# Gate O moves from the bank of I and F into the bank of G in the last LSTM steps, and the edge targets are loaded once

## The chip, the cores and the metric

The kernel runs on one core of one Trainium2 chip. TensorE (PE in the profile, with its weight loads as PEld), VectorE (DVE), ScalarE (ACT), GpSimd (POOL) and SyncE (SP) each work through a queue of their own in order, and wait for each other on counters (semaphores). The metric is the device time of one execution in microseconds; of a kernel, the median of its runs is taken.

## The reference

One layer of a graph network on 6250 nodes of 256 features with 100000 edges, all in float32. `x` is normalised, then three branches add up:

```
xn = layernorm(x)
x  = x + GIN(xn, src, dst) + MIX(xn)      # segment_sum(xn[src], dst), two matmuls, batch norm; linear attention, two matmuls
x  = x + FFN(layernorm(x))                # an LSTM over the 6250 rows, hidden size 256

def step(carry, xp):                      # the LSTM
    h, c = carry
    i, f, g, o = split(xp + h @ W_hh.T, 4)
    c = sigmoid(f) * c + sigmoid(i) * tanh(g)
    h = sigmoid(o) * tanh(c)
```

The LSTM's outputs then give logits, an argmax, and weighted prefix and suffix sums that are added to the outputs. `dst` is sorted.

## The kernel before, in words

**The start (lines 204 to 343).** Nodes are laid out as 125 chunks of 50 steps. `x` comes in six groups of steps (`LN_GROUPS`, L223, two DMAs each by `move`, L118) on SP's queue, is normalised on DVE, ACT and POOL (L270 to L296), and is written to `xn_d` in DRAM, again on SP's queue (L296). The edges are loaded on ACT's queue (L208 to L216): `src` and `dst` each as a tile of `rows_e` rows of `EP` = 7 blocks of 128 edges, 112 rows of 896, in the buffer `behind`, a part of the large buffer that is called "counts" in the profile. The last row has no more than 5 real blocks; one DMA (L215) fills the other two. PE turns these tiles so that each block of 128 edges is one column (`edges_to_partitions`, L239: an integer-to-float copy on ACT, 7 transposes, two copies). The targets are needed a second time in another shape, 98 rows of 1024 (two groups of 512 edges each), for the smallest and largest target of each group (`ends`, L321) and of each pair (`pairs`, L333). For this `dst` is loaded again on SP's queue (L225 to L230, six DMAs into `flat`, a part of `m2`). These stand in SP's queue after the loads of `x` and before the stores of `xn_d`. A DMA that is issued waits until the one that used the same of eight counters, eight DMAs before it over SP and ACT, has landed.

After that POOL gathers rows of `xn_d` by `src` (L376, 646 gathers of 128 rows); the first one waits for all stores of `xn_d`. The iota of L362 (392 columns, in "counts") is copied to PSUM by ACT (L364) and used at L371 and L609.

**The LSTM.** The 125 chunks run side by side, 50 steps each. After 40 warm-up steps and the first 10 real ones (L1180 to L1208), the real steps from `KEPT` = 10 to 49, 40 of them, are run by an order written by hand (L1235 to L1282: `manual_schedule`, in which PE, DVE and ACT keep the order of the code). The input parts of the gates of these steps lie in DRAM; SP fetches one step's three steps ahead (`fetch`, L1120).

Gates and features are split into two halves `a` of 128 features, and so is h (`k`). A step makes 16 products (`products`, L1229): for each gate and half `a`, one with each half `k` of the last h. They add to input parts that `bring` (L1221) has placed in PSUM beforehand: by PE for the first steps, then by copies on ACT. There are six tiles in PSUM: `bank_g[a]` for G alone, `pg_g` in the profile, and `bank_o[s % 2][a]` for I, F and O, `pg` in the profile, in two sets that change with the step. The order of a step on PE is: six products with h's half 0; G, I, F, O of half 0 with h's half 1; then the rest of half 1; then the logits of the step before (L954). On ACT: tanh of G half 0 (L1254), sigmoid of I, F and O of half 0 in one instruction of 375 columns (L1256), tanh of G half 1 (L1258), the next step's copy into `bank_g[0]`, tanh of c half 0 (L1268), sigmoid of I, F, O of half 1, the copies into `bank_g[1]` and `bank_o[1]`, and tanh of c half 1. On DVE, for each half: the multiply of I, F with G, c (L1265), the add (L1266), a weighted sum of an earlier step (L959), and h = o * tanh(c) (L1271); after half 1 also the sums over the outputs (L963, L968, L959). The first product of the next step waits for h half 0 (L1271), the seventh for h half 1.

In the warm-up and the first ten steps (`step`, L1125) all four gates of a half lie in one PSUM tile and ACT reads them one by one (L1140).

Of the kernel before, what the change touches and what calls it, by code (L numbers as in the profile page):

```python
# [14 lines left out]
F32 = mybir.dt.float32  # L15
I32 = mybir.dt.int32
BF16 = mybir.dt.bfloat16
AF = mybir.ActivationFunctionType
# [5 lines left out]
P = 128  # L24
N, D, E = 6250, 256, 100000


NC, NS = 125, 50
HEADS, HC = 8, 32
KD = D // P  # L30
NE = -(-E // P)


GT, W = 4, 96
GROUPS = -(-NE // GT)
GE = GT * P
# [54 lines left out]
def gps_layer(ctx: ExitStack, tc: tile.TileContext, x, src, dst, cols, rows, kvln, wqkv, mw1, mw2, gw1, gw2,  # L91
              wih, whh, blstm, out):
    nc = tc.nc
# [38 lines left out]
    m2 = big.tile([P, 2 * BANK * KD], F32, name="m2", tag="M2")  # L132
# [11 lines left out]
    with ExitStack() as s1:  # L144
# [3 lines left out]
        def edges_flat(t, start, ap):  # L148
            return bass.AP(tensor=t.tensor, offset=t.offset + start, ap=ap)


        EP = 7
        rows_e = -(-NE // EP)
        si = wp.tile([P, rows_e * EP], I32, name="si")
        base_i = wp.tile([1, GROUPS], I32, name="base_i")
# [47 lines left out]

        with tc.tile_pool(name="ln1", bufs=2) as lp, tc.tile_pool(name="ps0", bufs=6, space=PSUM) as ps:

            tiled = []
            left = NE - (rows_e - 1) * EP
            for i, t in enumerate((src, dst)):  # L208
                s = behind[:, i * EP * P:(i + 1) * EP * P].bitcast(I32)
                for r0, r1 in ((0, 96), (96, rows_e - 1)):  # L210
                    nc.scalar.dma_start(s[r0:r1], edges_flat(t, r0 * EP * P, [[EP * P, r1 - r0], [1, EP * P]]))
                nc.scalar.dma_start(s[rows_e - 1:rows_e, :left * P],
                                    edges_flat(t, (rows_e - 1) * EP * P, [[left * P, 1], [1, left * P]]))
                if left < EP:
                    nc.scalar.dma_start(s[rows_e - 1:rows_e, left * P:], edges_flat(t, 0, [[P, 1], [1, (EP - left) * P]]))  # L215
                tiled.append(s)  # L216

            rows_g = GROUPS // 2
            real = E - (rows_g - 1) * 2 * GE
            last = E - (GROUPS - 1) * GE  # L220
            flat = m2[:, :2 * GE].bitcast(I32)
            dg = flat.rearrange("p (j e) -> p j e", j=2)
            for s0, n in LN_GROUPS:  # L223
                move(nc.sync, xn[:, s0:s0 + n, :], by_step(x)[:, s0:s0 + n, :])
            nc.sync.dma_start(flat[:96, :], edges_flat(dst, 0, [[2 * GE, 96], [1, 2 * GE]]))  # L225
            nc.sync.dma_start(flat[96:rows_g - 1, :], edges_flat(dst, 96 * 2 * GE, [[2 * GE, rows_g - 97], [1, 2 * GE]]))
            nc.sync.dma_start(flat[rows_g - 1:rows_g, :real], edges_flat(dst, (rows_g - 1) * 2 * GE, [[real, 1], [1, real]]))
            for at in range(real, 2 * GE, last):
                n = min(last, 2 * GE - at)
                nc.sync.dma_start(flat[rows_g - 1:rows_g, at:at + n], edges_flat(dst, E - n, [[real, 1], [1, n]]))  # L230
            nc.gpsimd.iota(iota, pattern=[[1, W]], base=0, channel_multiplier=0,
                           allow_small_or_imprecise_dtypes=True)
            nc.gpsimd.iota(place, pattern=[[1, 2]], base=0, channel_multiplier=2,
# [4 lines left out]
            with tc.manual_schedule(engines={mybir.EngineType.PE, mybir.EngineType.DVE, mybir.EngineType.Activation}):  # L238
                def edges_to_partitions(i):  # L239

                    to = (si, drel)[i].rearrange("p (q j) -> p j q", j=EP)
                    f = m1[:, i * EP * P:(i + 1) * EP * P]

                    nc.scalar.copy(f[:rows_e], tiled[i][:rows_e])
                    for j0 in range(0, EP, 4):
                        n = min(4, EP - j0)
                        pt = ps.tile([P, BANK], F32, name="mm")
                        pt = pt[:, :n * rows_e].rearrange("p (j q) -> p j q", q=rows_e)
                        for j in range(n):
                            nc.tensor.transpose(pt[:, j, :], f[:rows_e, (j0 + j) * P:(j0 + j + 1) * P],  # L250
                                                ident[:rows_e, :rows_e])
                        nc.scalar.copy(to[:, j0:j0 + n, :], pt)
# [98 lines left out]
        ps = s1.enter_context(tc.tile_pool(name="ps1", bufs=4, space=PSUM))  # L351
# [13 lines left out]
        to = [sums[:, k, :N].rearrange("p (c s) -> p s c", s=NS) for k in range(KD)]  # L365
# [439 lines left out]
        with tc.manual_schedule(engines={mybir.EngineType.PE, mybir.EngineType.DVE, mybir.EngineType.Activation}):  # L805
# [5 lines left out]
            while slot < GROUPS - COUNTED or running or before or any(s >= slot for s in starts):  # L811
                g = slot + COUNTED
# [31 lines left out]
        with tc.If(held < GROUPS + PAIRS, preferred_fallthrough_block=False):  # L844
# [15 lines left out]
            with tc.For_i(0, NE, 1) as c:  # L860
                at = edge_p.tile([P, 1], I32, name="at1")
# [3 lines left out]
                g = gather(at[:, :1])  # L865
# [50 lines left out]
    I, F, G, O = range(4)  # L916

    SLOT = {I: 0, F: 1, O: 2, G: 3}
# [10 lines left out]
    gc = wl.tile([P, KD, 2, NC], F32, name="gc")  # L929
# [111 lines left out]
    with tc.tile_pool(name="lstm", bufs=2) as rp:  # L1041
        AHEAD, FETCH = 3, 3
        s2 = ExitStack()
        ps = s2.enter_context(tc.tile_pool(name="ps3", bufs=4, space=PSUM))
# [170 lines left out]
        s2 = ExitStack()  # L1215
        ps = s2.enter_context(tc.tile_pool(name="ps_k", bufs=1, space=PSUM))
        ps_y = s2.enter_context(tc.tile_pool(name="ps_l", bufs=2, space=PSUM))
        bank_g = [ps.tile([P, NC], F32, name=f"pg_g{a}") for a in range(KD)]
        bank_o = [[ps.tile([P, SLOT[G], NC], F32, name=f"pg{i}{a}") for a in range(KD)] for i in range(2)]

        def bring(s, t, gate_g, a):  # L1221

            to, of = (bank_g[a], t[:, a, SLOT[G], :]) if gate_g else (bank_o[s % 2][a], t[:, a, :SLOT[G], :])
            if s < KEPT + (1 if gate_g else 2):
                nc.tensor.matmul(to, ident, of, start=True, stop=False, skip_group_check=True)
            else:
                nc.scalar.copy(to, of)

        def products(s, *of):  # L1229
            for g, a, k in of:  # L1230
                to = bank_g[a] if g == G else bank_o[s % 2][a][:, SLOT[g], :]
                nc.tensor.matmul(to, w_hh[:, k, block(g, a)], of_step(s - 1)[:, k, :], start=False, stop=(k == KD - 1),  # L1232
                                 skip_group_check=True)

        with tc.manual_schedule(engines={mybir.EngineType.PE, mybir.EngineType.DVE, mybir.EngineType.Activation}):  # L1235
            t = fetched.pop(0)
            for gate_g in (False, True):
                for a in range(KD):
                    bring(KEPT, t, gate_g, a)
            fetched.append(fetch(KEPT + FETCH))  # L1240
            w = None
            for s in range(KEPT, NS):
                more = s + 1 < NS
                t = fetched.pop(0) if more else None
                if more:
                    bring(s + 1, t, False, 0)
                products(s, (G, 0, 0), (I, 0, 0), (F, 0, 0), (O, 0, 0), (I, 1, 0), (F, 1, 0))
                products(s, (G, 0, 1), (I, 0, 1), (F, 0, 1), (O, 0, 1))
                products(s, (G, 1, 0), (G, 1, 1), (O, 1, 0), (I, 1, 1), (F, 1, 1), (O, 1, 1))
                pl = ps_y.tile([P, BANK], F32, name="pl")[:, :NC]  # L1250
                logits(s - 1, pl)
                for a in range(KD):
                    if a == 0:
                        nc.scalar.activation(gc[:, 0, 0, :], bank_g[0], AF.Tanh)  # L1254
                    gates = rp.tile([P, 4, NC], F32, name="gates")[:, :SLOT[G], :]
                    nc.scalar.activation(gates, bank_o[s % 2][a], AF.Sigmoid)  # L1256
                    if a == 0:
                        nc.scalar.activation(gc[:, 1, 0, :], bank_g[1], AF.Tanh)  # L1258
                    if more:
                        bring(s + 1, t, True, a)  # L1260
                    if a and more:
                        bring(s + 1, t, False, 1)

                    two = rp.tile([P, 2, NC], F32, name="two", tag="h_w")
                    nc.vector.tensor_mul(two, gates[:, :2, :], gc[:, a])  # L1265
                    nc.vector.tensor_add(c[:, a, :], two[:, 0, :], two[:, 1, :])  # L1266
                    t_c = rp.tile([P, NC], F32, name="t_c")
                    nc.scalar.activation(t_c, c[:, a, :], AF.Tanh)  # L1268
                    if w is not None:
                        weighted(s - 2, 0, w, a)  # L1270
                    nc.vector.tensor_mul(of_step(s)[:, a, :], gates[:, SLOT[O], :], t_c)  # L1271
                if more:
                    w = summed(s - 1, rp, pl)
                else:
                    gated_part(s - 1, last_w[:, 0], pl)
                if s + 1 + FETCH < NS:
                    fetched.append(fetch(s + 1 + FETCH))
            for k in range(KD):
                weighted(NS - 2, 2, inc, k)
            pl = ps_y.tile([P, BANK], F32, name="pl")[:, :NC]  # L1280
            logits(NS - 1, pl)
            gated_part(NS - 1, last_w[:, 1], pl)  # L1282
# [38 lines left out]
    with tc.If(right < 2 * D * (NC - 1), preferred_fallthrough_block=False):  # L1321
# [12 lines left out]
        with tc.For_i(0, NC, 1) as c0:  # L1334
# [3 lines left out]
            pg = ps.tile([P, NG, NS], F32, name="pg1")  # L1338
# [96 lines left out]
```

## Time and profile before

| | |
|---|---|
| median of 17 runs | 1682.35 us (1678.57 to 1686.9) |
| the profiled execution | 1680.71 us, of which the span is 1678.9 us |
| PE busy | 1454.9 us, 87% of the span |
| DVE, ACT, POOL busy | 927.8, 650.6, 697.0 us |
| mean granted clock of PE | 0.939 |
| the last 40 LSTM steps | from 1450 to 1638 us of the span |
| first gather issued | 59.34 us |

The page lists, for each group of instructions, the line of the kernel, the engine, what is written from what, the count, the busy time with the mean duration of one in ns, and the idle time before the group with what ended it. Matmuls in float32 take two passes, so the 640 products of L1232 are 1280 instructions there. The timeline gives start and duration in us; in brackets the idle time of the engine before the instruction, and who ended it. The chain of waits follows the work back from what ended last.

### The profile page before, as it was taken

The page shows a single profiled execution, that of the slowest core. Times are in us where ns is not written, and L with a number is a line of the kernel's source. Part 1 is how long each engine was busy: PE and PEld are TensorE (multiplying, and loading weights), DVE is VectorE, ACT ScalarE, POOL GpSimd, SP SyncE. Part 2 cuts the span into 40 slices and gives each one's busy share as a digit, 9 for nine tenths or more (in the row PEclk, how much of TensorE's full clock was granted, in tenths as well). Part 3 has the DMA queues.
Part 4 walks back from the last instruction along what each step waited for, and adds up shares of the span by engine and source line. Part 5 has one row for each costly group of instructions (what it writes and reads, how often), then busy time and mean ns, then how long its engine had stood idle before and what let it go on. Part 6 is the DMA issues. An engine that isn't in the chain of part 4 may idle for free.

```text
span 1678.9 us, 30496 instructions
## 1 busy us (share of the span) xinstructions
PE 1454.9 (87%) x11064; PEld 1383.9 (82%) x11064; DVE 927.8 (55%) x2923; ACT 650.6 (39%) x1917; POOL 697.0 (42%) x752
## 2 busy tenths in 40 slices
PE   2478888988887888988988889799999999999995
PEld 2467787887787788887888888799999999988884
DVE  5577677777773122212222213566667665688887
ACT  4432333333330122212322222566666653466660
POOL 5466666666666666666566664000000000000006
PEclk9689899899998899999999999899999999999996
DMA  9623332233234344433333333211111110133324
GB/s 231 224 88 89 89 88 86 86 89 88 87 88 143 114 127 130 127 104 105 95 102 101 104 101 120 76 75 63 75 62 75 63 51 1 50 111 111 111 74 155
DMA packets 63623, 165.98 MB, mean 99 GB/s; under 512 B 14415, under 2 KB 27943, under 8 KB 62460
## 3 DMA queue, kind: packets, MB, share of 16 engines
q0 software_dynamic: 31008, 84.71, 17.1%
q1 hardware_dynamic: 32016, 78.37, 14.2%
q8 instruction: 91, 1.49, 0.4%
q10 hardware_dynamic: 436, 0.81, 0.2%
q14 instruction: 72, 0.59, 0.1%
HBM read 130.56 MB, written 33.28 MB: 98 GB/s over the span
## 4 chain that ended last, share of the span: by engine, by line
PE 68%; DVE 12%; issue 10%; ACT 4%; DMA 2%; another core or an unknown queue 2%; POOL 1%; SPq 1%; DVEq 0%; POOLq 0%; ACTq 0%
PE pg L397 15%; PE pg L1107 11%; PE pg L1131 10%; PE mm L582 6%; PE pg L1232 4%; PE mm L593 4%; PE mm L422 3%; PE mm L543 3%; PE sums_c L737 2%; PE mm L554 2%; PE pg_g L1232 2%; ACT gates L1256 1%; DVE counts L622 1%; DVE counts L609 1%
## 5 line engine op out<-in xcount | busy, mean ns | idle before, releaser
L376 POOL DMA_INDIRECT eg<-xn_d,si x646 | 618.1, 957 | 374.2 <-issue 143.2
L397 PE MATMUL pg<-here,eg 128*128 128x96 f32 x2584 | 412.7, 286 | 40.1 <-issue 36.3
L397 PEld LDWEIGHTS pg<-here,eg 128*128 128x128 f32 x2584 | 386.8, 207 | 57.8 <-issue 43.1
L407 DVE TENSOR_TENSOR sums<-sums,pg 128x192 f32 x162 | 57.5, 355 | 513.3 <-PE pg L397 285.4
L1107 PE MATMUL pg<-yT,w_ih 128*128 128x125 f32 x1600 | 190.0, 278 | 0.7 <-ACT yT L1098 0.7
L1107 PEld LDWEIGHTS pg<-yT,w_ih 128*128 128x128 f32 x1600 | 185.6, 194 | 1.3 <-ACT yT L1098 1.3
L582 PE MATMUL mm<-sums,g 128*128 128x125 f32 x800 | 133.5, 305 | 36.6 <-issue 23.8
L582 PEld LDWEIGHTS mm<-sums,g 128*128 128x128 f32 x800 | 117.3, 215 | 45.8 <-issue 38.5
L1073 POOL TENSOR_TENSOR ln_r<-ln_v,minus_half 125x1 f32<-125x1 f32 x50 | 26.8, 540 | 294.9 <-DVE ln_v L1067 294.9
L1131 PE MATMUL pg<-h_w,w_hh 128*128 128x125 f32 x1248 | 145.7, 275 | 0.0
L1131 PEld LDWEIGHTS pg<-h_w,w_hh 128*128 128x128 f32 x1248 | 142.5, 192 | 0.0
L598 ACT ACTIVATE sums<-mm,vec 128x125 f32<-128x125 f32 x100 | 30.9, 362 | 281.8 <-DVE sums L407 97.1
L1140 ACT ACTIVATE gates<-pg,b_l 128x125 f32<-128x125 f32 x398 | 111.5, 362 | 57.1 <-PE pg L1131 35.7
L1232 PE MATMUL pg<-sums,w_hh 128*128 128x125 f32 x960 | 126.8, 275 | 0.0
L422 PE MATMUL mm<-m,xr 128*125 128x256 f32 x400 | 113.8, 410 | 12.4 <-DVE counts L622 7.7
L593 PE MATMUL mm<-z,g 128*128 128x125 f32 x800 | 116.8, 282 | 4.4 <-issue 3.8
L1232 PEld LDWEIGHTS pg<-sums,w_hh 128*128 128x128 f32 x960 | 116.8, 192 | 0.0
L430 ACT ACTIVATE mm<-kv 125x512 f32<-125x512 f32 x50 | 30.1, 602 | 212.3 <-DVE kv L427 153.2
L1296 POOL TENSOR_TENSOR begin_h<-sums,begin_h 128x248 f32<-128x248 f32 x1 | 0.7, 710 | 261.3 <-DVE sums L1271 261.3
L593 PEld LDWEIGHTS mm<-z,g 128*128 128x128 f32 x800 | 102.5, 195 | 6.2 <-issue 5.2
L588 ACT ACTIVATE z<-mm,vec 128x125 f32<-128x125 f32 x200 | 56.5, 370 | 127.7 <-PE pg L397 88.5
L422 PEld LDWEIGHTS mm<-m,xr 128*125 128x125 f32 x400 | 75.4, 204 | 24.3 <-issue 8.5
(276 smaller groups left out, 2375.9 us busy)
## 6 DMA issues: line engine op xcount, KB each, us to landing
x_d<-x_out SPq DMA_DIRECT2D x40, 500.0 KB
x_in<-x_d SPq DMA_DIRECT2D x40, 500.0 KB
eg<-xn_d,si POOLq DMA_INDIRECT x646
counts<-xn_d SPq DMA_DIRECT2D x16, 384.0 KB
m<-in_x_dram SPq DMA_DIRECT2D x50, 112.0 KB
out_dram<-o SPq DMA_DIRECT2D x12, 448.0 KB
xn<-in_x_dram SPq DMA_DIRECT2D x4, 1120.0 KB
xn_d<-xn SPq DMA_DIRECT2D x4, 1120.0 KB
```

The costliest lines, as they stand in the source:

```text
L376: nc.gpsimd.indirect_dma_start(out=g, out_offset=None, in_=xn_d[:], in_offset=bass.IndirectOffsetOnAxis(ap=at, axis=0))
L397: nc.tensor.matmul(pg[:, k, :], g[:, k * P:(k + 1) * P], here[:, i, :], start=(i == 0 and k == 0), stop=(i == n - 1), skip_group_check=True)
L407: nc.vector.tensor_add(window, window, pg)
L422: nc.tensor.matmul(pkv[:r, at], xnT[:, j, k, :], w_qkv[:, k, D:][:, at], start=(k == 0 and half == 0), stop=(k == KD - 1), skip_group_chec ...
L543: nc.tensor.matmul(pu[:, m, :], w_qkv[:, k, m * P:(m + 1) * P], xnT[:, j, k, :], start=(m == 0 and k == 0), stop=(k == KD - 1), skip_group ...
L582: nc.tensor.matmul(p1[:, m, :], g1[:, k, m * P:(m + 1) * P], sums[:, k, at], start=(m == 0 and k == 0), stop=(k == KD - 1), skip_group_che ...
L588: nc.scalar.activation(z1[:, m, :], p1[:, m, :], AF.Relu, bias=col("gb1", m))
L593: nc.tensor.matmul(p2[:, a, :], g2[:, m, a * P:(a + 1) * P], z1[:, m, :], start=(a == 0 and m == 0), stop=(m == 2 * KD - 1), skip_group_ch ...
L1107: nc.tensor.matmul(pg[:, SLOT[g], :], w_ih[:, k, block(g, a)], yT[:, k, s * NC:(s + 1) * NC], start=(i == 0 and k == 0), stop=False, skip_ ...
L1131: nc.tensor.matmul(banks[a][:, SLOT[g], :], w_hh[:, k, block(g, a)], h[:, k, :], start=False, stop=(k == KD - 1), skip_group_check=True)
L1140: nc.scalar.activation(gate[g], pg[:, SLOT[g], :], AF.Tanh if g == G else AF.Sigmoid, bias=bias(g, a))
L1232: nc.tensor.matmul(to, w_hh[:, k, block(g, a)], of_step(s - 1)[:, k, :], start=False, stop=(k == KD - 1), skip_group_check=True)
```

## The change

In the last 40 steps, O moves from the tile of I and F (now `bank_i`, 250 columns) to that of G (`bank_g`, now O and G, 250 columns). `bring` copies 250 and 250 columns in place of 375 and 125. The products of O are issued later: O of half 0 after the first product of G half 1, and both of O half 1 last. The sigmoid becomes two instructions for each half, 250 columns for I and F and 125 for O.

At the start, `EP` becomes 8, so the tiles of `src` and `dst` have 98 rows of 1024, the shape that `ends` and `pairs` need. `flat` is now the tile of `dst` itself, and the second load on SP's queue goes away. The rest of the last row is filled from the padding behind the edges, 96 values at a time: three DMAs on ACT's queue for each of the two tensors.

```diff
-        EP = 7
+        EP = 2 * GT
...
+            rows_g = GROUPS // 2
             tiled = []
-            left = NE - (rows_e - 1) * EP
+            left, pads = (NE - (rows_e - 1) * EP) * P, NE * P - E
             for i, t in enumerate((src, dst)):
                 s = behind[:, i * EP * P:(i + 1) * EP * P].bitcast(I32)
                 for r0, r1 in ((0, 96), (96, rows_e - 1)):
                     nc.scalar.dma_start(s[r0:r1], edges_flat(t, r0 * EP * P, [[EP * P, r1 - r0], [1, EP * P]]))
-                nc.scalar.dma_start(s[rows_e - 1:rows_e, :left * P],
-                                    edges_flat(t, (rows_e - 1) * EP * P, [[left * P, 1], [1, left * P]]))
-                if left < EP:
-                    nc.scalar.dma_start(s[rows_e - 1:rows_e, left * P:], edges_flat(t, 0, [[P, 1], [1, (EP - left) * P]]))
+                nc.scalar.dma_start(s[rows_e - 1:rows_e, :left], edges_flat(t, (rows_e - 1) * EP * P, [[left, 1], [1, left]]))
+                for at in range(left, EP * P, pads):
+                    n = min(pads, EP * P - at)
+                    nc.scalar.dma_start(s[rows_e - 1:rows_e, at:at + n], edges_flat(t, E, [[n, 1], [1, n]]))
                 tiled.append(s)
-
-            rows_g = GROUPS // 2
-            real = E - (rows_g - 1) * 2 * GE
-            last = E - (GROUPS - 1) * GE
-            flat = m2[:, :2 * GE].bitcast(I32)
+            flat = tiled[1]
             dg = flat.rearrange("p (j e) -> p j e", j=2)
             for s0, n in LN_GROUPS:
                 move(nc.sync, xn[:, s0:s0 + n, :], by_step(x)[:, s0:s0 + n, :])
-            nc.sync.dma_start(flat[:96, :], edges_flat(dst, 0, [[2 * GE, 96], [1, 2 * GE]]))
-            nc.sync.dma_start(flat[96:rows_g - 1, :], edges_flat(dst, 96 * 2 * GE, [[2 * GE, rows_g - 97], [1, 2 * GE]]))
-            nc.sync.dma_start(flat[rows_g - 1:rows_g, :real], edges_flat(dst, (rows_g - 1) * 2 * GE, [[real, 1], [1, real]]))
-            for at in range(real, 2 * GE, last):
-                n = min(last, 2 * GE - at)
-                nc.sync.dma_start(flat[rows_g - 1:rows_g, at:at + n], edges_flat(dst, E - n, [[real, 1], [1, n]]))
...
-        bank_g = [ps.tile([P, NC], F32, name=f"pg_g{a}") for a in range(KD)]
-        bank_o = [[ps.tile([P, SLOT[G], NC], F32, name=f"pg{i}{a}") for a in range(KD)] for i in range(2)]
+        bank_g = [ps.tile([P, 2, NC], F32, name=f"pg_g{a}") for a in range(KD)]
+        bank_i = [[ps.tile([P, 2, NC], F32, name=f"pg{i}{a}") for a in range(KD)] for i in range(2)]
...
-            to, of = (bank_g[a], t[:, a, SLOT[G], :]) if gate_g else (bank_o[s % 2][a], t[:, a, :SLOT[G], :])
+            to, of = (bank_g[a], t[:, a, 2:, :]) if gate_g else (bank_i[s % 2][a], t[:, a, :2, :])
...
-                to = bank_g[a] if g == G else bank_o[s % 2][a][:, SLOT[g], :]
+                to = bank_g[a][:, SLOT[g] - 2, :] if g in (O, G) else bank_i[s % 2][a][:, SLOT[g], :]
...
-                products(s, (G, 0, 1), (I, 0, 1), (F, 0, 1), (O, 0, 1))
-                products(s, (G, 1, 0), (G, 1, 1), (O, 1, 0), (I, 1, 1), (F, 1, 1), (O, 1, 1))
+                products(s, (G, 0, 1), (I, 0, 1), (F, 0, 1))
+                products(s, (G, 1, 0), (O, 0, 1), (G, 1, 1), (I, 1, 1), (F, 1, 1), (O, 1, 0), (O, 1, 1))
...
-                        nc.scalar.activation(gc[:, 0, 0, :], bank_g[0], AF.Tanh)
+                        nc.scalar.activation(gc[:, 0, 0, :], bank_g[0][:, 1, :], AF.Tanh)
                     gates = rp.tile([P, 4, NC], F32, name="gates")[:, :SLOT[G], :]
-                    nc.scalar.activation(gates, bank_o[s % 2][a], AF.Sigmoid)
+
+                    nc.scalar.activation(gates[:, :2, :], bank_i[s % 2][a], AF.Sigmoid)
+                    nc.scalar.activation(gates[:, SLOT[O], :], bank_g[a][:, 0, :], AF.Sigmoid)
                     if a == 0:
-                        nc.scalar.activation(gc[:, 1, 0, :], bank_g[1], AF.Tanh)
+                        nc.scalar.activation(gc[:, 1, 0, :], bank_g[1][:, 1, :], AF.Tanh)
```

## The prediction

> **What bounds the kernel now.** I read the page first, then busy time by window, then the chain of waits and the timeline inside the stage that changes, and last the timeline of the first 60 us. The page:
>
> ```profile
> PE 68%; DVE 12%; issue 10%; ACT 4%; DMA 2%; another core or an unknown queue 2%; POOL 1%; SPq 1%; DVEq 0%; POOLq 0%; ACTq 0%
> ...
> L1232 PE MATMUL pg<-sums,w_hh 128*128 128x125 f32 x960 | 126.8, 275 | 0.0
> ```
>
> TensorE (PE) carries 68% of the chain. The second line would suggest that the changed LSTM steps (L1232) are pure PE work, with no idle time before it. Busy time by window (columns: PE, PEld, DVE, ACT, POOL, then granted clock) corrects that a little:
>
> ```profile
> 1500.00:1550.00 50.00, 47.47 (x388) 44.58 (x386) 42.12 (x130) 33.50 (x109) 0.00 (x0) 1.00 0.33 106
> ```
>
> PE is 95% busy at full clock, yet VectorE (DVE) is 84% busy beside it. The chain of waits, between two steps, says which of them leads:
>
> ```profile
> 1503.41 0.37 PE pg_g L1232 x2
> 1503.78 0.68 PE pg L1232 x6
> ...
> 1504.48 0.49 ACT gates L1256
> ...
> 1505.00 0.43 DVE two L1265
> ...
> 1505.45 0.30 DVE gc L1266
> ...
> 1505.78 0.32 ACT t_c L1268
> ...
> 1506.12 0.30 DVE sums L1271
> ...
> 1506.46 0.49 PE pg_g L1232 x2
> ```
>
> So a step is a loop: products, sigmoid, multiply, add, tanh of c, product with o, next step's products. It is a recurrence and not a throughput. One step takes 4.665 us (from 1501.81 to 1520.46 lie four), while its 18 products (16, and 2 for the logits) need 18 x 0.223 = 4.01 us (ten of them went from 1503.29 to 1505.52). The rest is PE waiting for h. What is later on this loop is paid in full, 40 times. ScalarE's (ACT) own order in that step, by the timeline:
>
> ```profile
> 1503.29 0.49 PE L1232 MATMUL pg_g<-sums,w_hh 128*128 128x125 f32 x2
> 1503.81 0.28 ACT L1254 ACTIVATE gc<-pg_g 128x125 f32<-128x125 f32 x1 [0.53 <-PE pg_g L1232]
> 1504.93 0.27 ACT L1258 ACTIVATE gc<-pg_g 128x125 f32<-128x125 f32 x1
> 1505.10 0.27 ACT L1227 COPY pg_g<-x_in 128x125 f32<-128x125 f32 x1
> 1505.99 0.46 ACT L1256 ACTIVATE gates<-pg 128x375 f32<-128x375 f32 x1
> 1506.35 0.27 ACT L1227 COPY pg_g<-x_in 128x125 f32<-128x125 f32 x1
> 1506.55 0.47 ACT L1227 COPY pg<-x_in 128x375 f32<-128x375 f32 x1
> ```
>
> Let t be the time since the first product with h's second half (1503.29). Then the tanh of G's half 0 starts at 0.52, the sigmoid of half 0 at 1.19, the tanh of G's half 1 at 1.64. A result is thus readable 0.30 after the n-th product is issued: 0.223 n + 0.30 gives 0.52 for n=1 (G), 1.19 for n=4 (O) and 1.64 for n=6. ACT takes 0.20 us from one start to the next after 125 columns and 0.36 after 375. How a bank is waited for is seen in an earlier step, where all four gates of a half lie in one PSUM tile:
>
> ```profile
> 1443.28 3.29 PE L1131 MATMUL pg<-sums,w_hh 128*128 128x125 f32 x28
> ...
> 1445.33 1.13 ACT L1140 ACTIVATE gates<-pg,b_l 128x125 f32<-128x125 f32 x4 [3.86 <-PE pg L1131]
> ```
>
> Gate I of that half was complete after 5 of its 8 products, readable at 1443.28 + 5 x 0.223 + 0.30 = 1444.70. ACT had been idle 3.86 us, and began at 1445.33, when the eighth was (1445.36 by the same rule). A reader waits for the last product of the tile.
>
> In the first 60 us, DMA leads:
>
> ```profile
> 29.02 3.16 SPq L230 DMA_DIRECT2D m<-in_dst_dram  x3
> ...
> 34.51 19.95 SPq L121 DMA_DIRECT2D xn_d<-xn  x12
> ...
> 49.94 2.33 DVE L333 TENSOR_REDUCE pairs<-m 17x4 f32<-17x1024 int32 x2
> ...
> 59.34 1.21 POOL L376 DMA_INDIRECT eg<-xn_d,si  x1 [13.07 <-issue]
> ```
>
> The first gather waits for the last store of xn_d. The stores stand in SyncE's (SP) queue behind the second load of dst, though the first group was normalised by 24.2.
>
> **The change, part by part.** *LSTM: what waits for what.* O now shares G's tile, and the order with h's second half is G0 I0 F0 G1 O0 G1 I1 F1 O1 O1. In the compiled changed program PE raises its counter twice per step, after the fifth of these (O0) and after the tenth (O1, the last); the tanh of G0 waits for the first, the tanh of G1 for the second, and the sigmoids carry no wait of their own, since the tanh ahead of them has it already. So the tanh of G0 moves from 0.52 to 0.223 x 5 + 0.30 = 1.41, and the tanh of G1 from 1.64 to 0.223 x 10 + 0.30 = 2.53. ACT is in order, and behind that second tanh are the copy of G/O for the next step and then the tanh of c0, which is on the loop.
>
> *Prices of the new shapes.* A 250-column ACT instruction reading PSUM takes 0.37 us (the copy at L1098, 128x250, 0.368). To the next start I take 0.28, midway between 0.20 and 0.36; those two are the ends. The copy of G/O half 1 waits for the end of the sigmoid of O1 just before it (a wait on ACT's own counter in the compiled program): 0.27 + 0.03 in place of 0.20.
>
> *The step, in t, before and after:*
> - tanh G0 0.52, now 1.41; sigmoid of half 0 1.19, now (I, F alone) 1.41 + 0.19 = 1.60.
> - Multiply on DVE: 1.71, now 1.60 + 0.37 + 0.04 = 2.01. Add: 0.45 later, 2.46; its result reaches ACT at 2.79.
> - ACT meanwhile: sigmoid O0 at 1.88, tanh G1 at 2.53, copy G/O at 2.72, free at 3.00. The tanh of c0 goes from 2.49 to 3.00: 0.21 of that is the copy.
> - h half 0: tanh + 0.34 = 3.34, PE has it at 3.68 (before 3.17).
> - Sigmoid of half 1: tanh c0 + 0.21 = 3.21 (before 2.70); multiply 3.62 (3.20), add 4.07, tanh c1 4.40 (3.97). ACT in between: sigmoid O1 3.49, copies at 3.79 and 4.07, free 4.35, so just not in the way.
> - h half 1 4.75 (4.32), and the next step's first second-half product 0.34 later: 5.09 (4.66).
>
> The loop grows by 0.43 us. With 0.20 for the 250-column start the same working gives 5.00 (+0.34); with 0.36 the two copies end at 4.67, hold up the tanh of c1, and the step is 5.36 (+0.70). I take 0.43: 39 steps and 0.16 in the last, which has no copies: **+17 us** (ends +13.5 and +28). PE's work is the same 18 products. The 80 added sigmoids, 0.27 each or 22 us of ACT time, lie in its gaps; the price above is of order. DVE does the same and gets later with the loop.
>
> *The Trainium skill on that.* "PSUM — Partial Sum Buffer", section "PSUM bank collisions raise a hardware error", asks to guard PSUM by bank and quadrant, not by address. The warm-step row above agrees (1445.33, not 1444.70). By that rule the sum is the one above; by waits on addresses it would be the first rival's.
>
> *dst loaded once: SP.* Six DMAs leave SP's queue ahead of the stores (L225 to L230, 0.40 MB, issued from 22.71 to 32.18). At the 253 GB/s of the first 62 us 0.40 MB is 1.6 us of transfer. The DMA share is 0.79 at 32 to 34 us and 0.53 at 34 to 36, some 1.3 us empty, which stores of the groups that are ready at 24.2 and 29.6 would fill. After 44 us the queue is full, so both come off the last store: **-3 us**. Ends: -6.5, where POOL's iota (below) becomes the gate at 52.8 in place of 59.34; and +0.5, if the third group's load, which in the new order waits for dst's load (landed 11.4; that load was issued at 10.90), is held up and nothing is gained.
>
> *What moves and is hidden.* Each tensor's last row gets three pad DMAs in place of one: 4 more issues on ACT's queue at 0.27 us, 1.1 us in all, ahead of a square root at 13.24 that ACT awaits idle for 1.14; beyond that the DVE waits until 17.97 for x anyway. The cast becomes 98x1024 (0.92 x 1024/896 = 1.05 us, +0.13, twice), one more transpose of 0.22 us per tensor: beside loads that end at 29. The dst tile is now kept until the reductions at L321 and L333, and the iota of L362 writes over it: POOL runs it at 10.04 before, and now only after L333 (52.27), to 52.7. Behind it in POOL's queue stand the gathers, and ACT's copy iota_p (0.49) to 53.2 stands before L370, which waits for the stores like the gathers. The cover is the stores, due at 55 or later; without it, the iota is the gate named above.
>
> **Sum.** Against the profiled execution, 1680.71 us (span 1678.9 and 1.8 around it): 1680.7 + 17 - 3 = 1694.7. It stands 1.64 below the median of 1682.35; carried over, 1696.
>
> **Rivals.** *Waits by address (faster).* If the tanh of G0 were released by its own product, the sigmoid of I and F would start at 0.223 x 3 + 0.30 = 0.97, multiply at 1.38, tanh c0 at 2.16, h half 1 at 3.90 and the step take 4.24: -0.42 x 40 = -17, with the prologue -20, 1662. It decides from the point where the tanh of G0 starts before 1.11 (the old multiply at 1.71, less 0.04, 0.37 and 0.19) and that of G1 before 2.02 (the old tanh of c0 at 2.49, less 0.28 and 0.19). For it: nothing in the arithmetic needs O there. Against: the counter raised only twice, and the warm step. *ACT becomes the bound.* The +0.70 end: 1682 + 28 - 3 = 1707. For it: the margin ahead of the tanh of c1 is 0.05 us. Against: ACT starts after 125 and 375 columns overlap their predecessors in every row above. *PE hides it.* 95% busy, so a later ACT might be covered: only the prologue counts, 1679. Against: the chain alternates through ACT and DVE, and PE waits for DVE in every step. *The stores gain nothing:* 1682 + 17 = 1699; it lies in the range.
>
> **How the numbers follow.** The forecast with its ends: 0.80 (1688 to 1704; the stores' rival is in it); ACT the bound: 0.10; PE hides it: 0.05; waits by address: 0.05. Likeliest: 1696. The range 1687 to 1705 holds the forecast, and leaves out the first and last rivals and most of the ACT one. A difference under 0.2% (3.4 us) can't be told from none here. Faster: 0.05 and half of 0.05, 0.07. Same: 0.04. Slower: 0.89.
>
> **What would show it.** Right: tanh of gc half 0 about 1.4 us after the first second-half product, waiting for PE, the second one about 2.5 us; the LSTM step near 5.1 us; PE idle before the first product of each step up from 0.23 to about 0.7 us; stores of xn_d from about 25 to 33 us, the first gather at 55 to 57, the iota near 52.5. Wrong: a tanh at 0.5, copies on ACT running nose to tail, a gather phase that does not keep its head start (a clock granted later at its start would do that).

## The result, and the profile after

The changed kernel takes 1699.57 us (median of 6 runs, 1696.9 to 1702.19), the kernel before 1682.36 (34 runs). The ratio is 1.0101, with a 95% interval of 1.009 to 1.0113: 17.2 us slower. 1696 was forecast, in a range of 1687 to 1705.

The profiled executions are 1680.71 us before and 1694.14 after, 13.4 us apart; the one after is the fastest execution of that kernel. Where these 13.4 us lie can be read from four points of the two traces:

| us from the span's start | before | after | difference |
|---|---|---|---|
| first gather | 59.34 | 54.70 | -4.6 |
| first product of the LSTM's input part (`w_ih`, L1107, after L1098) | 1064.13 | 1059.09 | -5.0 |
| from the first to the last h of the last 40 steps | 183.42 | 201.60 | +18.2 |
| end of the span | 1678.92 | 1692.36 | +13.4 |

So the start gained 4.6 us, the 1000 us of gathers kept that and added 0.4, the 40 steps lost 18.2, and the stretch behind the last h is longer by 0.4.

The page of the kernel after: the chain by engine, and the products into G's tile in the changed stage (idle time before the group behind the second bar), and then the same products before, by the list of groups:

```profile
PE 68%; DVE 11%; issue 9%; ACT 4%; another core or an unknown queue 3%; DMA 3%; POOL 1%; DVEq 0%; ACTq 0%; SPq 0%; POOLq 0%
...
L1223 PE MATMUL pg_g<-sums,w_hh 128*128 128x125 f32 x640 | 109.9, 284 | 31.0 <-DVE sums L1264 31.0
```

```profile
L1232 PE MATMUL pg_g<-sums,w_hh 128*128 128x125 f32 x320 | 62.9, 299 | 8.8 <-DVE sums L1271 8.8
```

The chain's shares hardly move, so they would not have told the story. The group does: it now has 31.0 us of idle time before it, ended by `sums` (h), where G's products had 8.8 before. The line of before with 0.0 that the prediction shows is the group of I, F and O; the wait for h never stood there, since G's product is the first of a step. Busy time of the same window as before (PE, PEld, DVE, ACT, POOL, granted clock, DMA share, GB/s):

```profile
1500.00:1550.00 50.00, 42.00 (x350) 40.13 (x350) 38.41 (x119) 30.39 (x117) 0.00 (x0) 1.00 0.31 96
```

PE is busy for 42.00 of 50 us (47.47 before), at full clock in both, and every other engine does less in the same time as well. Nothing became busier: the loop became longer. The chain of waits through one step of after:

```profile
1509.92 0.46 PE pg_g L1223 x4
1510.38 0.02 issue
1510.40 0.02 ACTq L1251
1510.42 0.04 issue
1510.46 0.28 ACT gc L1251
1510.74 0.27 ACT pg_g L1218
1511.01 0.24 ACT t_c L1261
1511.24 0.02 issue
1511.27 0.30 DVE sums L1264
1511.57 0.04 issue
1511.61 0.48 PE pg_g L1223 x2
```

Before, the chain left PE after the products of half 0 and went through sigmoid, multiply and add. Now it stays on PE to the very last product (1509.92), and then goes through three instructions in ACT's order: the tanh of G half 1 (L1251), the copy of G and O for the next step (L1218), and the tanh of c half 0 (L1261). Two of these have nothing to do with c half 0. They only stand ahead of it. The timeline of the next step (start, duration; in brackets the engine's idle time before it and who ended that):

```profile
1513.00 0.30 PEld L1223 LDWEIGHTS pg_g<-sums,w_hh 128*128 128x128 f32 x2
...
1514.42 0.28 ACT L1245 ACTIVATE gc<-pg_g 128x125 f32<-128x125 f32 x1 [1.53 <-PE pg_g L1223]
...
1514.59 0.37 ACT L1248 ACTIVATE gates<-pg 128x250 f32<-128x250 f32 x1
...
1514.85 0.28 ACT L1249 ACTIVATE gates<-pg_g 128x125 f32<-128x125 f32 x1
...
1515.00 0.42 DVE L1258 TENSOR_TENSOR two<-gates,gc 128x250 f32<-128x250 f32 x1 [0.56 <-ACT gates L1248]
...
1515.45 0.29 DVE L1259 TENSOR_TENSOR gc<-two 128x125 f32<-128x125 f32 x1
1515.60 0.28 ACT L1251 ACTIVATE gc<-pg_g 128x125 f32<-128x125 f32 x1 [0.47 <-PE pg_g L1223]
...
1515.77 0.37 ACT L1218 COPY pg_g<-x_in 128x250 f32<-128x250 f32 x1
1516.07 0.30 ACT L1261 ACTIVATE t_c<-gc 128x125 f32<-128x125 f32 x1
...
1516.75 0.48 PE L1223 MATMUL pg_g<-sums,w_hh 128*128 128x125 f32 x2 [0.80 <-DVE sums L1264]
```

The weights of the first product with h's second half are loaded from 1513.00 on; t counts from there, here and below (in the prediction's step this load and the product both stand at 1503.29). The tanh of G half 0 starts at t = 1.42 (0.53 before), that of half 1 at 2.60 (1.64 before), the tanh of c half 0 at 3.07 (2.49 before). ACT is idle for 1.53 us before the first of them and for 0.47 before the second, both ended by PE.

At the start, the stores of `xn_d` as SP issues them, and then POOL's iota and first gather:

```profile
24.92 24.84 SPq L121 DMA_DIRECT2D xn_d<-xn  x12
```

```profile
53.26 0.46 POOL L353 IOTA counts<- 128x392 f32 x1 [5.04 <-DVE ope L327]
54.70 1.21 POOL L367 DMA_INDIRECT eg<-xn_d,si  x1 [0.98 <-issue]
```

The stores begin at 24.92 (34.51 before), and the DMA engines are no longer empty at 32 to 36 us: their share, second number from the end, was 0.79 and 0.53 there before and is now

```profile
32.00:34.00 2.00, 2.00 (x15) 2.00 (x14) 1.97 (x12) 1.75 (x4) 1.85 (x4) 1.00 0.98 399
34.00:36.00 2.00, 2.00 (x22) 2.00 (x21) 0.32 (x1) 2.00 (x5) 1.41 (x3) 1.00 0.91 384
```

The iota, freed late by the reductions of the targets, ends at 53.72, just ahead of the first gather, so the trace alone does not tell whether it or the stores now let the gathers start.

### The profile page after: what moved, and what is told of

Read it like the earlier page. It is cut to its first block, busy times and chain, and to the rows that moved or that the text cites. A ratio compares the mean times of both kernels' runs of the same rounds, so it can differ in the third digit from the quotient of the medians.

```text
span 1692.4 us, 30612 instructions
## 1 busy us (share of the span) xinstructions
PE 1449.9 (86%) x11066; PEld 1379.5 (82%) x11066; DVE 927.9 (55%) x2923; ACT 652.2 (39%) x1997; POOL 698.7 (41%) x752
## 4 chain that ended last, share of the span: by engine, by line
PE 68%; DVE 11%; issue 9%; ACT 4%; another core or an unknown queue 3%; DMA 3%; POOL 1%; DVEq 0%; ACTq 0%; SPq 0%; POOLq 0%
PE pg L388 13%; PE pg L1098 11%; PE pg L1122 10%; PE mm L573 5%; PE pg_g L1223 5%; PE pg L1223 4%; PE mm L584 4%; PE mm L413 4%; PE mm L534 3%; PE sums_c L728 2%; PE mm L545 2%; DVE counts L613 1%; DVE counts L600 1%; DVE sums L398 1%
## 5 line engine op out<-in xcount | busy, mean ns | idle before, releaser
L388 PE MATMUL pg<-here,eg 128*128 128x96 f32 x2584 | 408.1, 285 | 33.8 <-issue 19.7
L388 PEld LDWEIGHTS pg<-here,eg 128*128 128x128 f32 x2584 | 382.2, 206 | 52.2 <-issue 36.3
L1098 PE MATMUL pg<-yT,w_ih 128*128 128x125 f32 x1600 | 189.7, 277 | 0.7 <-ACT yT L1089 0.7
L1098 PEld LDWEIGHTS pg<-yT,w_ih 128*128 128x128 f32 x1600 | 185.2, 194 | 1.3 <-ACT yT L1089 1.3
L1223 PE MATMUL pg_g<-sums,w_hh 128*128 128x125 f32 x640 | 109.9, 284 | 31.0 <-DVE sums L1264 31.0
L1223 PEld LDWEIGHTS pg_g<-sums,w_hh 128*128 128x128 f32 x640 | 87.1, 191 | 38.6 <-DVE sums L1264 38.5
L413 PEld LDWEIGHTS mm<-m,xr 128*125 128x125 f32 x400 | 77.3, 209 | 26.1 <-issue 13.5
```

Source lines behind the costliest of these rows:

```text
L388: nc.tensor.matmul(pg[:, k, :], g[:, k * P:(k + 1) * P], here[:, i, :], start=(i == 0 and k == 0), stop=(i == n - 1), skip_group_check=True)
L413: nc.tensor.matmul(pkv[:r, at], xnT[:, j, k, :], w_qkv[:, k, D:][:, at], start=(k == 0 and half == 0), stop=(k == KD - 1), skip_group_chec ...
L1098: nc.tensor.matmul(pg[:, SLOT[g], :], w_ih[:, k, block(g, a)], yT[:, k, s * NC:(s + 1) * NC], start=(i == 0 and k == 0), stop=False, skip_ ...
```

## The experiments

The theory: a reader of a PSUM tile waits for the last product into the whole tile, so O, issued late, holds back the two tanh of G that share its tile; ACT's order carries the delay to the tanh of c. The main rival once the result was known: the 80 added ACT instructions and their order on ACT cost the time by themselves. The experiments were run on two chips, e1 to e4 on one and e5 to e8 on another. The kernel before takes 1519.42 us on the one (17 runs, 1515.16 to 1522.12) and 1670.48 on the other (17 runs, 1666.03 to 1674.63), so each ratio is against the kernel before on the same chip, run beside it. What the traces show of the changed steps, in t, and of the start:

| kernel | step, us | tanh G half 0, half 1 | multiply half 0 | h half 0, half 1 | first gather at |
|---|---|---|---|---|---|
| before | 4.662 | 0.53, 1.64 | 1.71 | 2.83, 4.32 | 59.34 |
| after | 5.133 | 1.42, 2.60 | 2.00 | 3.40, 4.79 | 54.70 |
| e1, LSTM part alone | 5.130 | 1.42, 2.60 | 2.00 | 3.40, 4.79 | 62.07 |
| e2, start alone | 4.661 | 0.53, 1.64 | 1.71 | 2.83, 4.32 | 57.03 |
| e3, O in its own tile | 4.230 | 0.53, 1.74 | 1.38 | 2.50, 3.88 | 56.16 |
| e4, O's products early | 4.408 | 1.20, 2.09 | 1.50 | 2.62, 4.07 | 56.04 |
| e5, after again | 5.131 | 1.42, 2.60 | 2.00 | 3.40, 4.79 | 57.31 |
| e6, only O half 0 early | 5.130 | 0.75, 2.60 | 1.61 | 3.40, 4.79 | 57.32 |
| e7, only O half 1 early | 4.842 | 1.42, 2.15 | 2.00 | 3.12, 4.50 | 55.78 |
| e8, iota freed early | 5.130 | 1.42, 2.60 | 2.00 | 3.40, 4.79 | 56.41 |

**e1: the LSTM part alone.** The kernel before, with the second half of the diff only (L1209 to L1253 of after); `EP` and the loads at the start stay as before.

> The kernel before, with only the LSTM part of the change. Theory (the tanhs of G wait for O's products, the loop of a step grows): a step of 5.13 us as in the changed kernel, against 4.665, times 40: +18 us, ratio 1.0107. Rival (the loss was made elsewhere, for instance in the gather phase, and the LSTM part costs less than the trace of one execution shows): +10 us or less.

Measured: 1536.22 us (5 runs), ratio 1.0113 (1.0096 to 1.013), +17 us. The step is the changed kernel's to 0.003 us. The LSTM part is the whole loss.

**e2: the start alone.** The kernel before, with the first half of the diff only (`EP`, the pads, `flat = tiled[1]`, no second load on SP).

> The kernel before, with only the single load of dst (EP = 8). Theory (the head start of the first gather, 54.7 against 59.34 us, is kept to the end): -4.6 us, ratio 0.9973. Rival (the gather phase gives it back in most executions, which would explain that the median of the changed kernel rose by 17 us and its profiled execution by 13): between -1 and +1 us, with the first gather still near 54.7.

Measured: 1516.12 us (12 runs), ratio 0.9981 (0.9969 to 0.9993), a gain of 3 us with 1 to 5 as its interval. The first gather is at 57.03, against 62.07 in e1, which has the old start on the same chip. The expected size lies just inside the interval; e1 and e2 together give +14.

**e3: O in a tile of its own.** G, I with F, and O have one tile for each half, six in all; for that the second set of I and F is given up, and each copy into a tile stands behind the last reader of that tile.

```diff
-        bank_g = [ps.tile([P, 2, NC], F32, name=f"pg_g{a}") for a in range(KD)]
-        bank_i = [[ps.tile([P, 2, NC], F32, name=f"pg{i}{a}") for a in range(KD)] for i in range(2)]
+        bank = {G: [ps.tile([P, NC], F32, name=f"pg_g{a}") for a in range(KD)],
+                I: [ps.tile([P, 2, NC], F32, name=f"pg{a}") for a in range(KD)],
+                O: [ps.tile([P, NC], F32, name=f"pg_o{a}") for a in range(KD)]}
...
-                products(s, (G, 0, 0), (I, 0, 0), (F, 0, 0), (O, 0, 0), (I, 1, 0), (F, 1, 0))
+                products(s, (G, 0, 0), (I, 0, 0), (F, 0, 0), (I, 1, 0), (F, 1, 0), (O, 0, 0))
...
-                    nc.scalar.activation(gates[:, SLOT[O], :], bank_g[a][:, 0, :], AF.Sigmoid)
                     if a == 0:
-                        nc.scalar.activation(gc[:, 1, 0, :], bank_g[1][:, 1, :], AF.Tanh)
-                    if more:
-                        bring(s + 1, t, True, a)
+                        if more:
+                            bring(s + 1, t, G, 0)
+                            bring(s + 1, t, I, 0)
+                        nc.scalar.activation(gc[:, 1, 0, :], bank[G][1], AF.Tanh)
+                    nc.scalar.activation(gates[:, SLOT[O], :], bank[O][a], AF.Sigmoid)
...
```

> The changed kernel with O in PSUM tiles of its own: G, I/F and O each have one tile for each half (I and F lose their second set, so their copies for the next step stand behind this step's sigmoid). Theory (a reader waits for the last product of the tile): the tanh of G half 0 starts 0.52 us after the first second-half product, the multiply at 1.38, the step takes 4.25 us: (4.25 - 5.13) x 40 = -35 us against the changed kernel, so some 1664 us. Rival (ACT with its 80 more sigmoids is what is too slow): ACT has more instructions still, so the step stays at 5.1 us or gets longer, 1699 us or more.

Measured: 1500.13 us (4 runs), ratio 0.9882 (0.9861 to 0.9902), 18 us faster than before by the ratio. ACT in one step of e3, by its timeline, and busy time by window:

```profile
1350.16 0.28 ACT L1244 ACTIVATE gc<-pg_g 128x125 f32<-128x125 f32 x1 [0.73 <-PE pg_g L1224]
1350.61 0.38 ACT L1246 ACTIVATE gates<-pg 128x250 f32<-128x250 f32 x1 [0.17 <-PE pg L1224]
1350.88 0.27 ACT L1219 COPY pg_g<-x_in 128x125 f32<-128x125 f32 x1
1351.07 0.37 ACT L1219 COPY pg<-x_in 128x250 f32<-128x250 f32 x1
1351.37 0.28 ACT L1251 ACTIVATE gc<-pg_g 128x125 f32<-128x125 f32 x1
1351.54 0.27 ACT L1252 ACTIVATE gates<-pg_o 128x125 f32<-128x125 f32 x1
1351.80 0.31 ACT L1262 ACTIVATE t_c<-gc 128x125 f32<-128x125 f32 x1
...
1354.38 0.28 ACT L1244 ACTIVATE gc<-pg_g 128x125 f32<-128x125 f32 x1 [0.73 <-PE pg_g L1224]
```

```profile
1300.00:1350.00 50.00, 50.00 (x428) 48.91 (x427) 45.60 (x143) 39.44 (x167) 0.00 (x0) 1.00 0.37 123
```

The tanh of G half 0 starts after one product again (0.53), the sigmoid of I and F after three, and the tanh of c half 0 at 1351.80, which is t = 2.17 (t counts from 1349.63 here). The next step's tanh comes 4.22 us after this one, and PE now reads as busy for the whole window. ACT has 167 instructions in 50 us, more than the 117 of after, and 2077 in all against 1997: more ACT work, and the fastest step. That answers the rival as far as the number of instructions goes; e3 changes their order on ACT too, and e7 below takes away 0.29 us of the 0.47 that the step grew by with that order as it is. e3 keeps the split sigmoid and the late products of O: these are no loss, once O's products hold back O's reader alone.

**e4: the tiles of after, another order.** O stays in G's tile, but its products come before those of I and F half 1, and I and F half 0 come first; on ACT the copy goes ahead of the tanh of G half 1.

```diff
-                products(s, (G, 0, 1), (I, 0, 1), (F, 0, 1))
-                products(s, (G, 1, 0), (O, 0, 1), (G, 1, 1), (I, 1, 1), (F, 1, 1), (O, 1, 0), (O, 1, 1))
+                products(s, (I, 0, 1), (F, 0, 1), (G, 0, 1), (O, 0, 1))
+                products(s, (G, 1, 0), (G, 1, 1), (O, 1, 0), (O, 1, 1), (I, 1, 1), (F, 1, 1))
...
-                    if a == 0:
-                        nc.scalar.activation(gc[:, 0, 0, :], bank_g[0][:, 1, :], AF.Tanh)
...
                     nc.scalar.activation(gates[:, :2, :], bank_i[s % 2][a], AF.Sigmoid)
-                    nc.scalar.activation(gates[:, SLOT[O], :], bank_g[a][:, 0, :], AF.Sigmoid)
                     if a == 0:
-                        nc.scalar.activation(gc[:, 1, 0, :], bank_g[1][:, 1, :], AF.Tanh)
+                        nc.scalar.activation(gc[:, 0, 0, :], bank_g[0][:, 1, :], AF.Tanh)
+                    nc.scalar.activation(gates[:, SLOT[O], :], bank_g[a][:, 0, :], AF.Sigmoid)
                     if more:
                         bring(s + 1, t, True, a)
+                    if a == 0:
+                        nc.scalar.activation(gc[:, 1, 0, :], bank_g[1][:, 1, :], AF.Tanh)
```

> The changed kernel, same tiles, other order: products with h's second half I0 F0 G0 O0 G1 G1 O1 O1 I1 F1; on ACT the sigmoid of I and F first, and the tanh of G half 1 behind the copy of half 0. Theory: sigmoid at 0.75, tanh of G half 0 at 1.19, multiply at 1.51, tanh of G half 1 at 2.1 to 2.2, tanh of c0 at 2.35, step 4.45 us: -27 us against the changed kernel, some 1672. Rival (ACT's added instructions are the cause, not what they wait for): the step stays near 5.1 us, 1699.

Measured: 1504.44 us (4 runs), ratio 0.9917 (0.9894 to 0.9941), a step of 4.408. Against the tiles of before, the sharing need not cost anything, if the products into the shared tile end before those that others wait for; e3, without sharing, is still 0.18 us a step faster. The tanh of G half 1 starts at 2.09; its tile is complete after the 8th product, by the rule 0.223 x 8 + 0.30 = 2.08.

**e5: the changed kernel again**, on the chip of e6 to e8, as their common base.

> The changed kernel itself, beside the next three on one chip. Theory (the two parts add up: +0.47 us in each of 40 steps, and a head start of 4.6 to 5 us that is kept): +14 us against the kernel before. Rival (the head start is lost again in the gather phase): +18 us or more.

Measured: 1685.96 us (6 runs), ratio 1.0081 (1.0064 to 1.0098), that is +13.5 us by the ratio and +15.5 between the two medians.

**e6: only O half 0 early.** One product moves from fifth to second place among those with h's second half.

```diff
-                products(s, (G, 0, 1), (I, 0, 1), (F, 0, 1))
-                products(s, (G, 1, 0), (O, 0, 1), (G, 1, 1), (I, 1, 1), (F, 1, 1), (O, 1, 0), (O, 1, 1))
+                products(s, (G, 0, 1), (O, 0, 1), (I, 0, 1), (F, 0, 1))
+                products(s, (G, 1, 0), (G, 1, 1), (I, 1, 1), (F, 1, 1), (O, 1, 0), (O, 1, 1))
```

> The changed kernel, with O's product of half 0 issued second instead of fifth among those with h's second half (G0 O0 I0 F0 G1 G1 I1 F1 O1 O1); nothing else. Theory (a tanh of G waits for the tile's last product, and the tanh of G half 1, behind the very last product, holds up the tanh of c0 on ACT): the tanh of G half 0 starts at 0.75 in place of 1.42, the multiply at 1.60 in place of 2.00, yet the tanh of c0 stays at 3.07 and the step at 5.13: 0 us against the changed kernel. Rival (each of the two waits costs its own delay): the step falls by 0.4 us, -16 us. Rival (the tanh of G waits for its own product alone): the tanh does not move.

Measured: 1683.91 us (4 runs), ratio 1.007 (1.005 to 1.009); its interval and that of e5 overlap widely. The timeline of e6:

```profile
1502.40 0.28 ACT L1245 ACTIVATE gc<-pg_g 128x125 f32<-128x125 f32 x1 [0.86 <-PE pg_g L1223]
...
1503.26 0.42 DVE L1258 TENSOR_TENSOR two<-gates,gc 128x250 f32<-128x250 f32 x1 [0.17 <-ACT gates L1248]
...
1504.25 0.28 ACT L1251 ACTIVATE gc<-pg_g 128x125 f32<-128x125 f32 x1 [0.86 <-PE pg_g L1223]
1504.42 0.37 ACT L1218 COPY pg_g<-x_in 128x250 f32<-128x250 f32 x1
1504.72 0.30 ACT L1261 ACTIVATE t_c<-gc 128x125 f32<-128x125 f32 x1
...
1505.06 0.29 DVE L1264 TENSOR_TENSOR sums<-gates,t_c 128x125 f32<-128x125 f32 x1 [0.79 <-ACT t_c L1261]
```

The first tanh comes 0.67 earlier (t = 0.75, counted from 1501.66, which is 0.223 x 2 + 0.30), the multiply 0.39 earlier (1.61, since the sigmoid still has to wait for F, the fourth product), and the step does not move (5.130). The 0.39 us have become idle time in front of the second tanh, whose bracket grows from 0.47 to 0.86, ended by PE. Of two waits on one path, taking away the earlier alone gains nothing.

**e7: only O half 1 early.** Both products of O half 1 go ahead of I and F of half 1, so that G's and O's tile of half 1 is complete after eight products instead of ten.

```diff
-                products(s, (G, 1, 0), (O, 0, 1), (G, 1, 1), (I, 1, 1), (F, 1, 1), (O, 1, 0), (O, 1, 1))
+                products(s, (G, 1, 0), (O, 0, 1), (G, 1, 1), (O, 1, 0), (O, 1, 1), (I, 1, 1), (F, 1, 1))
```

> The changed kernel, with both products of O half 1 issued ahead of I1 and F1 (G0 I0 F0 G1 O0 G1 O1 O1 I1 F1); nothing else. Theory: the tanh of G half 0 stays at 1.42, that of half 1 moves from 2.60 to 2.15, the tanh of c0 from 3.07 to 2.80 where it meets its data, and the step from 5.13 to 4.87: -10 us against the changed kernel. Rival (the ACT work, not this wait, holds the tanh of c0): step at 5.13, 0 us.

Measured: 1674.02 us (10 runs), ratio 1.0019 (1.0006 to 1.0032), 12 us below e5 by the medians, with a step 0.289 shorter, or 11.6 us over 40 steps. The timeline of e7:

```profile
1504.04 0.28 ACT L1245 ACTIVATE gc<-pg_g 128x125 f32<-128x125 f32 x1 [1.53 <-PE pg_g L1223]
...
1504.77 0.28 ACT L1251 ACTIVATE gc<-pg_g 128x125 f32<-128x125 f32 x1
...
1504.94 0.37 ACT L1218 COPY pg_g<-x_in 128x250 f32<-128x250 f32 x1
...
1505.07 0.29 DVE L1259 TENSOR_TENSOR gc<-two 128x125 f32<-128x125 f32 x1
...
1505.39 0.31 ACT L1261 ACTIVATE t_c<-gc 128x125 f32<-128x125 f32 x1
```

Only products on PE have moved; ACT's instructions and their order are those of after (t counts from 1502.62 here). The second tanh no longer waits for long (no bracket), and the copy behind it leaves ACT free for a new start 0.30 later, at 1505.24. The tanh of c half 0 starts at 1505.39, 0.32 after the add (1505.07): now the first wait, through sigmoid, multiply and add, is what comes last. The step is 0.18 longer than before for that reason. e6 and e7 together show the two waits as two branches of which the later one counts. Both edits in one kernel were not tried.

**e8: the iota freed early.** The tiles of `src` and `dst` change places in the buffer, so that the iota no longer writes over the tile that the reductions still read.

```diff
-                s = behind[:, i * EP * P:(i + 1) * EP * P].bitcast(I32)
+                s = behind[:, (1 - i) * EP * P:(2 - i) * EP * P].bitcast(I32)
```

> The changed kernel with the tiles of src and dst in swapped places of the buffer, so that the iota of POOL writes over src, which is read early, and no longer waits for the reductions over dst: it runs at some 15 us in place of 53 to 55. Theory (the stores of xn_d are the gate of the first gather, the iota ends beside them): the first gather moves by less than 1 us, 0 us in all. Rival (the iota is the gate): the first gather comes 2 us or more earlier, and so does the end.

Measured: 1685.68 us (4 runs), ratio 1.0088 (1.0068 to 1.0108), the same as e5. POOL's timeline of e8, then of e5:

```profile
14.82 0.46 POOL L353 IOTA counts<- 128x392 f32 x1 [4.74 <-ACT m L235]
...
56.41 1.21 POOL L367 DMA_INDIRECT eg<-xn_d,si  x1 [6.99 <-DMA m<-in_wqkv_dram]
```

```profile
55.15 0.46 POOL L353 IOTA counts<- 128x392 f32 x1 [4.68 <-DVE ope L327]
57.31 1.21 POOL L367 DMA_INDIRECT eg<-xn_d,si  x1 [1.70 <-DMA m<-in_wqkv_dram]
```

The iota moves from 55.15 to 14.82, the first gather by 0.9 us only. The brackets name a load of weights (`in_wqkv`), which the gather doesn't need; it follows the stores in SP's queue and raises a counter that one of the stores has used. By the counters' own events in the traces, the last store lands at 56.16 in e5 and at 55.23 in e8, and the first gather starts 1.15 and 1.18 us later; in the trace of after the store lands at 53.55, the iota ends at 53.72, and the gather again starts 1.15 after the store. So the stores are the gate, in after too. The iota ends close beside them, and would probably take up a further gain of the stores unless it is moved as well; that was not tried.

**The better version.** e3 beats both kernels: 0.9882 of the time before, with a step of 4.230 us against 4.662 and 5.133. Its 18 products need 4.01 us of that by the prediction's 0.223 each.

## Why the prediction was right, step by step

*What bounds the kernel.* The reading as a recurrence holds. 17 us were added although PE does the same 18 products in a step, and PE's busy time in the window fell from 47.47 to 42.00. PE's idle time before the first product of a step went from 0.23 to 0.80 (about 0.7 was foreseen). Two small slips changed nothing: the line with 0.0 idle time was read for all products, and the step of 4.665 is 18.65 / 4 = 4.66.

*What waits for what.* Right, to 0.01 us at the first wait: the tanh of G half 0 starts at 1.42 (1.41 predicted). e6 (after two products, 0.75), e4 (after eight, 2.09) and e3 (own tile, 0.53) move it or its partner as the last product into the tile is moved. (The rule 0.223 n + 0.30 is right; it means 0.30 after the n-th product's 0.223 are over, not after its issue.) The step that the prediction worked out for its rival without this wait, 4.24, is what e3 takes with a tile for each, 4.23. In "PSUM — Partial Sum Buffer", section "PSUM bank collisions raise a hardware error", the Trainium skill asks to guard PSUM by bank; the waits found here agree, since the tanh in after reads G alone and still waits for O.

*The second tanh.* 2.53 was predicted, 2.60 measured. This is the term that was mis-sized, by 0.07 us. In the chain of after, 0.02 of issue, 0.02 of a separate instruction on ACT's queue (ACTq L1251) and 0.04 of issue stand between the product and this tanh. In the kernel before (6 products, 1.64) and in e4 (8 products, 2.09), it starts where the rule puts it; in e6, with the same order on ACT as after, it stands at 2.60 again, and in e7 at 2.15 against 2.08, though there ACT's sigmoid of O also ends only 0.02 before it. In the compiled program of these three the tanh carries two waits, for PE and for ACT's own counter, and the one for PE has an instruction of its own. The Trainium skill's "Perfetto Trace Analysis", section "Identifying Dependency Chains", says that extra semaphore instructions may stand ahead of an instruction that waits on multiple engines. That the 0.07 is this instruction was not tried by itself.

*The rest of the loop.* Copy at 2.77 (2.72), tanh of c half 0 at 3.07 (3.00), h half 0 at 3.40 (3.34), h half 1 at 4.79 (4.75), step 5.13 (5.09): the 0.07 is passed on, and 0.04 of it arrives. The loop grew by 0.47 and not by 0.43, 18.2 us instead of 17. The 250-column price, taken as 0.28 between ends of 0.20 and 0.36, was 0.26 after the sigmoid (1514.59 to 1514.85) and 0.30 after the copy (1515.77 to 1516.07).

*The start.* -3 was predicted, from the empty DMA time at 32 to 36 us. The first gather moved by -4.6 in the first pair of traces and -5.0 between e1 and e2; timed alone, the start is worth 3 us with an interval of 1 to 5. So the term was right within what can be timed, and by the traces somewhat small. What was foreseen as the lower end, the iota as a gate, came close (it ends at 53.72 and not 52.7) and does not decide (e8).

*The sum.* Predicted 1694.7 against the profiled execution, which took 1694.14: -4.6 and +18.2 in place of -3 and +17. By these traces both terms were too small, by 1.6 and 1.2 us, and the misses nearly cancel; that the sum is off by 0.6 only is luck. The median is 3.6 us above the forecast of 1696, since the other executions of after lie 0.9 to 8.1 us above the profiled one. The two fastest, 1694.14 (the profiled one) and 1695.03, are not among the six of the median; over all eight it is 1698.66, or 16.3 us above the kernel before. In e5's comparison the same pair differs by a ratio of 1.0081 (1.0064 to 1.0098), and its interval and the first one (1.009 to 1.0113) overlap from 1.009 to 1.0098, or 15.1 to 16.5 us of 1682; the traces give 13.4, and e1 and e2 together 14. Why the first comparison lies at the upper edge of this is open.

*The rivals.* Waits by address: refuted by the 1.42. ACT as the bound: refuted by e3, which gives ACT more to do and is faster, and by e7, which leaves ACT's work as it is and is faster than after; but the margin ahead of the tanh of c half 1 was as thin as the prediction said. PE hides it: refuted by e1, whose LSTM part alone costs 17 us, and by the window of 42.00. The stores gain nothing: refuted by e2, whose interval excludes 1.

## What to carry to other kernels

When gates or tiles are regrouped in PSUM, ask for each reader which product into its tile is issued last, and what stands behind that reader in its engine's order: an operand that nobody needs yet, placed in the tile of one that is needed first, delays everything behind. Of two waits on one loop, price the later one, and expect nothing from removing the earlier. A stage in which PE reads 95% busy, and whose largest group of products has 0.0 idle time before it, may still be a recurrence: the wait stood in a smaller group, and the chain through one step shows it.

## What the runs showed that was not expected

The kernel before takes 1519 us beside e1 to e4, 1670 beside e5 to e8 and 1682 in the first comparison. The steps of the last 40 agree to 0.003 us, and the difference lies in one phase: from the first gather to the first product of the LSTM's input part the kernel before needs 1004.8 us in the first profile (59.34 to 1064.13), the changed kernel in e5 994 (57.31 to 1051.42), and e1 and e2 844 to 845 (62.07 to 906.27, and 57.03 to 902.06). From 100 to 600 us PE is busy for 424 us in the first profile of before and for 475 in e2, and its granted clock there is 0.92 and 0.98. How much of it comes from the gathers and how much from the clock was not tried. The 40 steps are not touched by it, but between two chips the same program differs by some ten times what the change does.
